# One level of a blocked triangular inverse moved from TensorE to VectorE in a gated delta-rule kernel

## The chip, the cores and the metric

The kernel runs on one core of a Trainium2 chip. The metric is the device time of one execution in microseconds (us). All of the model is one launch; intermediate results that change their partition layout go through scratch tensors in DRAM.

## The reference, cut to what matters

The program is a chain of six residual blocks over 1024 tokens of width 256: a feed-forward block, windowed attention, two more feed-forward blocks, the gated delta-rule attention ("L1 attention") and a last feed-forward block. The change lies in the delta-rule attention, whose core is a scan over tokens, in 16 heads of 128 by 128 state:

```
q = l2norm(silu(conv(x @ Wq))) * DK**-0.5      # k likewise, v without the norm
g = exp(-softplus(x @ Wfa @ Wfb + dt_bias) * exp(A_log))
beta = sigmoid(x @ Wb)
def step(S, (qt, kt, vt, gt, bt)):
    S = S * gt[..., None]
    pred = einsum('bhk,bhkv->bhv', kt, S)
    delta = (vt - pred) * bt[..., None]
    S = S + kt[..., None] * delta[:, :, None, :]
    return S, einsum('bhk,bhkv->bhv', qt, S)
```

The kernel doesn't scan token by token. It takes chunks of 128 tokens. Inside a chunk the deltas solve a lower triangular system: with M the strictly lower matrix of decayed products of keys with keys, and the betas on the diagonal, delta = Z (v - k S), where Z is the inverse of the unit triangular matrix, scaled. Most of the kernel's second half is the making of M and of Z for each chunk and head.

## The kernel before

**Pairs.** The 16 heads are taken in 4 groups of 4 heads (`HG`), the 8 chunks in 4 pairs. That makes 16 pairs; a pair is one group of heads over 256 tokens, so it holds 2 chunks times 4 heads = 8 triangular matrices of 128 by 128.

**Stages of a pair,** each a Python generator whose `yield`s cut it into steps:

- `prepare`: convolutions of k and q (matmul L641, ScalarE L653, VectorE L655), their norms, the gates, and the products `kq` (L741, L742). It writes the betas over the norms, `cf`, to DRAM as `cfd` (L687), in elements of 4 bytes.
- `triangle`: M by levels n = 1, 2, 4, ... 64. A level makes the blocks of n rows below the diagonal blocks of n columns (matmul L791, L803), masks them into tiles (L854, L856, L857, or ScalarE copies), and moves the decay one level on (VectorE L813, GpSimd L819). Levels 1 to 8 go into the tile `ml`, level 16 into `mt16`, level 32 into `mt32`, level 64 into `mt64`. In the step of level 32, `ml` is written to DRAM as `dm` (L843, four transfers).
- `solve`: the 64 diagonal blocks of 16 by 16 (8 matrices times 8 blocks) are fetched from `dm` with one block per partition, `xb` (L888, eight transfers of 8 partitions), scaled to `nb` (L899), and inverted by substitution on VectorE (L906 to L934). `zb` and its transpose `ztb` are written into two DRAM tensors `z` and `zt` (L949, sixteen transfers), which are read back with rows on partitions (L951, L954, six transfers).
- `invert`: levels 16 and 32 on TensorE with the same code: `pmz` = M^T z (L968), negated by ScalarE to `mz` (L976), two products `dz` (L983, L991), copied into `z` and `zt` (VectorE L1008, L1010 at level 16; ScalarE L1014, L1016 at level 32). Then level 64 (L1020, L1024, L1028, L1031).
- `values` and `gates`: v and the output gate.
- `advance` and `emit`: the state's recurrence over the two chunks of the pair (L1046 to L1078), the norm, and the output projection into `x` (L1085 to L1104). `advance` needs the pair's finished `zt` at `pw` (L1052).

**The order of the work.** The loop over i works on four pairs at once: `prepare` on pair i+2, `triangle` on pair i+1, `solve`, `invert`, `values`, `gates` on pair i, `advance` and `emit` on pair i-1. `weave` merges their steps: a lane (begin, end, n, steps) spreads n steps evenly between two fractions of the iteration. That merged order is what the program states; the framework then plans the engines' queues against a simulated timeline with priorities from that order, so an engine may take a later step early when the plan finds it idle. What it plans is fixed: on the chip each engine works through its queue in order. All DMAs are issued by one queue, SP's (SyncE).

**Buffers that matter.** The DRAM tensors `z` and `zt` and the tile `ml` exist twice, by parity of the pair (`turns`). Outside the blocks that are written they stay zero from the start. The pool `blk` (`diag`, `xb`, `nb`, `zb`, `ztb`) has one buffer each.

Of the kernel before, what the change touches and what calls it, by code (L numbers as in the profile page):

```python
# [10 lines left out]
F32 = mybir.dt.float32  # L11
# [497 lines left out]
def delta_rule(tc, a, x, xnT, pp, bc, kon, ones, kdw, first):  # L509
# [33 lines left out]
    with ExitStack() as ctx:  # L543
# [57 lines left out]
        for i in range(2):  # L601
            turn = {}
            for nm in ("ml", "mt16", "mt32"):
                turn[nm] = cst.tile([P, 2, HG, 64], F32, name=f"{nm}_{i}")
                nc.gpsimd.memset(turn[nm], 0.0)
            for nm in ("z", "zt"):
                turn[nm] = dram.tile([2, HG, P, P], F32, name=f"{nm}_{i}", bufs=1)
                for c in range(2):
                    for r in range(2):
                        nc.sync.dma_start(  # L610
                            out=turn[nm][c].rearrange("h r s -> r h s")[:, :, 64 * r : 64 * r + 64],
                            in_=turn["mt16"][:, c],
                        )
# [159 lines left out]
        def triangle(us):  # L773
# [11 lines left out]
            for i, n in enumerate(LEVELS):  # L785
# [43 lines left out]
                if n == 32:  # L829
# [8 lines left out]
                    for c, u in enumerate(us):  # L838

                        dm = u["dm"] = dram.tile([HG, P + 1, 64], F32, name="dm", bufs=4)  # L840
                        for half in (lo, hi):
                            r0 = half.start + half.start // 64
                            nc.sync.dma_start(  # L843
                                out=dm[:, r0 : r0 + 64, :].rearrange("h r s -> r h s"), in_=turn["ml"][half, c]
# [8 lines left out]
                if n < BLK:  # L853
                    nc.vector.copy_predicated(dst(flat(turn["ml"])), pred4, run4(pm[:, 0]))  # L854
                else:
                    nc.vector.tensor_mul(dst(flat(turn["mt16"])), run4(pm[:, 0]), run4(all_heads(mask)))  # L856
# [15 lines left out]
        def blocks(ap):  # L872
# [3 lines left out]
                tensor=ap.tensor, offset=ap.offset, ap=[[BLK * (pitch + 1), P // BLK], [pitch, BLK], [1, BLK]]  # L876
            )

        def solve(us, vb):
# [5 lines left out]
            for c, u in enumerate(us):  # L885
                for h in range(HG):
                    q0 = 32 * c + 8 * h
                    nc.sync.dma_start(  # L888
                        out=xb[q0 : q0 + 8].rearrange("b (i j) -> b i j", j=BLK),
                        in_=blocks(u["dm"][h]),  # L890
                    )
# [49 lines left out]
            )  # L941
            z = us[0]["z2"] = lev.tile([P, 2, HG, 64], F32, name="z", bufs=1)
            zt = us[0]["zt2"] = lev.tile([P, 2, HG, P], F32, name="zt", bufs=2)
            for c, u in enumerate(us):
                for got, to in ((zb, "z"), (ztb, "zt")):
                    full = u["p"]["turn"][to][c]
                    for h in range(HG):
                        q0 = 32 * c + 8 * h
# [312 lines left out]
```

## Time and profile before

| | |
|---|---|
| time, median of 3 runs | 1785.18 us (1783.14 to 1787.38) |
| the profiled execution | 1795.66 us, its span 1793.8 us |
| TensorE busy | 1532.6 us (85%), in 13152 matmul records (an f32 matmul leaves two) |
| VectorE busy | 1186.9 us (66%) |
| ScalarE busy | 831.3 us (46%) |
| GpSimd busy | 526.4 us (29%) |
| mean granted TensorE clock | 0.897 |
| DMA | 54.94 MB in 150348 packets, 116784 of them under 512 B |

In the page and in the answers below, PE is TensorE's matmul, PEld its weight load, DVE VectorE, ACT ScalarE, POOL GpSimd, SP SyncE. A group's row has the line, engine, operation, names (out<-in), shapes and count, then busy us and mean ns of one, then the engine's idle time just before it with what ended most of it. A row of waits has who waited for what, then us in total, how many times, and the longest. A row of the timeline has start, duration, engine, line, operation, names, shapes, count, and in brackets the idle time before it with its releaser. A row of windows has the stretch, its length, busy time of each engine with its number of instructions, granted clock (PEclk), DMA share and GB/s. The delta-rule attention runs from about 585 us to 1732 us of the span; the pairs follow each other there from about 664 us.

### The profile page before, as it was taken

What the parts mean: (1) busy time and instruction counts of PE and PEld (TensorE: products, weight loads), DVE (VectorE), ACT (ScalarE), POOL (GpSimd) and SP (SyncE); (2) the same over time, 40 slices, a digit from 0 to 9 for tenths busy, and PEclk for the clock granted to TensorE, in tenths of its full rate; (3) what the DMA queues carried; (4) which work ended last, traced back from release to release, by engine and by line L of the source; (5) the groups of instructions that cost most, each with busy time, mean ns of one, the idle gap of its engine ahead of it and who ended that gap; (6) DMA issues with size and microseconds to landing.
All of it is one profiled execution on the core that took longest, in us unless ns stands there. A gap on an engine that the chain in (4) does not pass through costs nothing.

```text
span 1793.8 us, 33380 instructions
## 1 busy us (share of the span) xinstructions
PE 1532.6 (85%) x13152; PEld 1107.1 (62%) x13152; DVE 1186.9 (66%) x2569; ACT 831.3 (46%) x1981; POOL 526.4 (29%) x470
## 2 busy tenths in 40 slices
PE   7886868777999766789989889898999898998879
PEld 3434445545555555667767677677778776776745
DVE  3999977584232357667678678876768877877221
ACT  2117273746122344536645645654665564563320
POOL 0022223231001034335434434433434442543100
PEclk9997989889999766789889989989889988989989
DMA  7020000002002001021111121102120120111100
GB/s 241 32 54 26 3 19 1 1 1 66 0 0 47 1 7 23 10 52 28 24 15 43 21 56 22 30 12 44 38 50 15 22 47 9 40 24 23 56 0 24
DMA packets 150348, 54.94 MB, mean 31 GB/s; under 512 B 116784, under 2 KB 142704, under 8 KB 149936
## 3 DMA queue, kind: packets, MB, share of 16 engines
q1 hardware_dynamic: 150192, 52.81, 12.8%
q8 instruction: 104, 1.70, 0.4%
q14 instruction: 52, 0.43, 0.1%
HBM read 39.11 MB, written 11.70 MB: 28 GB/s over the span
## 4 chain that ended last, share of the span: by engine, by line
PE 41%; DVE 26%; ACT 11%; DMA 9%; issue 6%; POOL 4%; SPq 3%; another core or an unknown queue 1%; DVEq 0%; POOLq 0%; ACTq 0%
PE ps L641 5%; DMA dm<-ml 4%; PE po L160 4%; PE pg L135 3%; PE pu L135 3%; DVE kq L813 3%; ACT e L319 3%; PE pm L791 2%; PE pr L253 2%; DVE k L655 2%; PE pg L700 2%; PE px L1101 2%; DVE other L195 2%; PE po L365 2%; DVE other L208 2%
## 5 line engine op out<-in xcount | busy, mean ns | idle before, releaser
L819 POOL TENSOR_TENSOR k<-k,d 128x512 f32<-128x512 f32 x96 | 149.7, 1559 | 312.2 <-PE pm L791 190.6
L791 PE MATMUL pm<-kq,k 128*64 128x64 f32 x3072 | 133.5, 235 | 29.9 <-POOL kq L742 11.5
L791 PEld LDWEIGHTS pm<-kq,k 128*64 128x64 f32 x3072 | 113.3, 146 | 62.0 <-issue 40.0
L813 DVE TENSOR_TENSOR kq<-kq,d 128x1024 f32<-128x1024 f32 x96 | 130.8, 1363 | 17.8 <-PE pm L791 6.7
L319 ACT ACTIVATE e<-ps,nm 128x128 f32<-128x128 f32 x256 | 91.5, 397 | 63.6 <-DVE nm L314 62.3
L655 DVE SCALAR_TENSOR_TENSOR k<-ps,pp,k 128x256 f32<-128x256 f32 x192 | 84.7, 473 | 27.0 <-ACT k L653 25.5
L655 DVE SCALAR_TENSOR_TENSOR q<-ps,pp,q 128x256 f32<-128x256 f32 x192 | 86.2, 478 | 22.7 <-ACT q L653 20.0
L655 DVE SCALAR_TENSOR_TENSOR v<-ps,pp,v 128x256 f32<-128x256 f32 x192 | 87.5, 474 | 19.8 <-ACT v L653 18.5
L253 PE MATMUL pr<-xnT,wq 128*128 128x512 f32 x128 | 64.7, 641 | 22.1 <-DVE nm L314 10.6
L641 PE MATMUL ps<-xnT,wv 128*128 128x259 f32 x256 | 79.5, 439 | 2.7 <-DVE v L655 1.5
L983 PE MATMUL dz<-mz,zt 64*64 64x32 f32 x768 | 74.9, 230 | 8.0 <-ACT mz L976 8.0
L991 PE MATMUL dz<-zt,mz 64*64 64x32 f32 x1024 | 81.4, 234 | 0.0
L641 PE MATMUL ps<-xnT,wq 128*128 128x259 f32 x256 | 78.6, 442 | 0.4 <-DVE ss L681 0.2
L365 PE MATMUL po<-wo,oT 128*128 128x256 f32 x256 | 64.1, 394 | 13.7 <-ACT oT L362 12.4
L991 PEld LDWEIGHTS dz<-zt,mz 64*64 64x64 f32 x1024 | 67.3, 147 | 12.4 <-issue 10.6
L1101 PE MATMUL px<-wdo,oT 128*128 128x256 f32 x256 | 70.4, 421 | 5.1 <-ACT oT L1097 5.1
L641 PE MATMUL ps<-xnT,wk 128*128 128x259 f32 x256 | 71.8, 418 | 1.0 <-ACT k L653 0.5
L742 POOL TENSOR_TENSOR kq<-q,ge 128x1024 f32<-128x1024 f32 x16 | 51.3, 3209 | 70.3 <-PE pso L1073 40.0
L653 ACT ACTIVATE q<-ps,pp 128x256 f32<-128x256 f32 x64 | 30.4, 474 | 89.1 <-PE ps L641 86.5
L968 PE MATMUL pmz<-z,mt 64*64 64x64 f32 x1024 | 56.1, 233 | 18.0 <-DMA z<-z 13.7
L968 PEld LDWEIGHTS pmz<-z,mt 64*64 64x64 f32 x1024 | 42.9, 140 | 44.4 <-issue 17.8
L708 ACT ACTIVATE gy<-pg,pp 128x256 f32<-128x256 f32 x64 | 29.4, 474 | 85.4 <-PE pg L700 67.5
(215 smaller groups left out, 3953.5 us busy)
## 6 DMA issues: line engine op xcount, KB each, us to landing
zt<-zt SPq DMA_DIRECT2D x32, 256.0 KB
dm<-ml SPq DMA_DIRECT2D x64, 64.0 KB
z<-z SPq DMA_DIRECT2D x64, 64.0 KB
wq<-in_aWq SPq DMA_DIRECT2D x1, 2048.0 KB
wo<-in_aWo SPq DMA_DIRECT2D x1, 2048.0 KB
wk<-in_dWk SPq DMA_DIRECT2D x4, 512.0 KB
wq<-in_dWq SPq DMA_DIRECT2D x4, 512.0 KB
wv<-in_dWv SPq DMA_DIRECT2D x4, 512.0 KB
```

What stands on the lines that cost most here:

```text
L135: nc.tensor.matmul(ps[:n], lhsT=w[:, c, cs], rhs=xnT[:, c, cols], start=(c == 0), stop=(c == KC - 1))
L253: nc.tensor.matmul(pr, lhsT=w[:, c, hcol : hcol + HD], rhs=xnT[:, c, PAD + hf * 512 : PAD + (hf + 1) * 512], start=(c == 0), stop=(c == KC ...
L319: nc.scalar.activation(e[:, s, j, :], ps[:, s, j, :], AF.Exp, bias=nm[:, 4 * s + j : 4 * s + j + 1], scale=SUB**-0.5, accum_out=z[:, s, j ...
L365: nc.tensor.matmul(po, lhsT=oT[:, h, :], rhs=wpool["wo"][:, g * HG + h, :], start=(h == 0), stop=(h == HG - 1),)
L641: nc.tensor.matmul(ps[:, 0 : 2 * P + 3], lhsT=w[nm][:, c, h * HD : (h + 1) * HD], rhs=xnT[:, c, PAD + t0 - 3 : PAD + t0 + 2 * P], start=(c ...
L655: nc.vector.scalar_tensor_tensor(yh, xi, pp[:, col : col + 1], yh, ALU.mult, ALU.add)
L791: nc.tensor.matmul(pm[half, :, c * HG + h, :].rearrange("p b (s l) -> p b s l", l=n), lhsT=k[:, c, h, half], rhs=rights(kq[:, :, c, h, half]),
L813: nc.vector.tensor_mul(kqr, kqr, dl.unsqueeze(1).unsqueeze(3).to_broadcast([P, 2, 2 * HG * runs, n]),)
L819: nc.gpsimd.tensor_mul(kl, kl, dr.unsqueeze(2).to_broadcast([P, 2 * HG * runs, n]))
L968: nc.tensor.matmul(pmz[half, c, h], lhsT=p["turn"][f"mt{n}"][half, c, h], rhs=z[half, c, h], start=True, stop=True,)
L991: nc.tensor.matmul(runs(dz[half, 1, c, h]), lhsT=mz[half, c, h], rhs=right(zt[half, c, h, half], n), start=True, stop=True,)
L1101: nc.tensor.matmul(px, lhsT=oT[:, h, :], rhs=u["w"]["o"][:, h, :], start=(h == 0), stop=(h == HG - 1))
```

## The change

Level 16 of the inverse leaves TensorE. Each of the 64 pairs of neighbouring 16 by 16 blocks becomes 32 joins (8 matrices times 4), and VectorE makes them right behind the substitution, on 128 partitions: 32 joins times 4 quarters of the columns. For a join with diagonal inverses z1, z2 and the block m of M between them, the new block is -z2 m z1.

- `mt16` is gone; level 16 of M is masked into `ml` with a copy like levels 1 to 8, so that it reaches DRAM in `dm`, which now comes behind level 16.
- `dm` is one tensor for both chunks, with a pitch that lets one access pattern step through all blocks: `xb` is one transfer instead of eight. Four more transfers fetch the blocks m, once for each quarter, into `mb` (rows of 16 floats, 64 B).
- At the end of `solve`, z1 (a quarter of the columns of `ztb`) and z2 are copied from SBUF to SBUF onto the 128 partitions (eight transfers), and `zb` and `ztb` are written to DRAM in one transfer each.
- A new stage `join` has two products and two reductions on VectorE over 1024 elements each, two small ScalarE operations for the sign, and eight transfers that write the new blocks into `zt` (rows of 64 B) and `z` (rows of 4 floats, 16 B). The six transfers that read `z` and `zt` back follow it.
- `invert` keeps level 32 (in its own short code) and level 64: 5 steps instead of 8.
- The lanes get other places.

```diff
@@ delta_rule @@
-            for nm in ("ml", "mt16", "mt32"):
+            for nm in ("ml", "mt32"):
...
-                turn[nm] = dram.tile([2, HG, P, P], F32, name=f"{nm}_{i}", bufs=1)
+                turn[nm] = dram.tile([2 * HG, P + 1, P], F32, name=f"{nm}_{i}", bufs=1)
...
@@ triangle @@
-                        dm = u["dm"] = dram.tile([HG, P + 1, 64], F32, name="dm", bufs=4)
+                    dm = us[0]["dm"] = dram.tile([2 * HG, P + 2, 64], F32, name="dm", bufs=2)
...
-                if n < BLK:
-                    nc.vector.copy_predicated(dst(flat(turn["ml"])), pred4, run4(pm[:, 0]))
-                else:
-                    nc.vector.tensor_mul(dst(flat(turn["mt16"])), run4(pm[:, 0]), run4(all_heads(mask)))
+                nc.vector.copy_predicated(dst(flat(turn["ml"])), pred4, run4(pm[:, 0]))
@@ solve @@
-            for c, u in enumerate(us):
-                for h in range(HG):
-                    q0 = 32 * c + 8 * h
-                    nc.sync.dma_start(
-                        out=xb[q0 : q0 + 8].rearrange("b (i j) -> b i j", j=BLK),
-                        in_=blocks(u["dm"][h]),
-                    )
+            dm = us[0]["dm"]
+            nc.sync.dma_start(
+                out=xb.rearrange("b (i j) -> b i j", j=BLK),
+                in_=blocks(dm, (BLK, BLK, 64), (1, 0, BLK), (0, 1, BLK)),
+            )
+            mb = blk.tile([P, BLK, BLK], F32, name="mb")
+            for j in range(4):
+                nc.sync.dma_start(
+                    out=mb[32 * j : 32 * j + 32],
+                    in_=blocks(dm, (32, 32, 32), (1, 0, BLK), (0, 1, BLK), col=BLK),
+                )
...
+            for j in range(4):
+                at = slice(32 * j, 32 * j + 32)
+                nc.sync.dma_start(out=z1[at], in_=ztb[0:64:2, 4 * j : 4 * j + 4, :])
+                nc.sync.dma_start(out=z2[at], in_=zb[1:64:2])
+            rows = ((BLK, BLK, 64), (1, 0, BLK), (0, 1, BLK))
+            for got, to in ((zb, "z"), (ztb, "zt")):
+                nc.sync.dma_start(out=blocks(us[0]["p"]["turn"][to], *rows), in_=got)
+            us[0]["blocks"] = mb, z1, z2
+            yield
@@ join, new @@
+            nc.vector.tensor_mul(
+                four,
+                mb.rearrange("p r s -> p s r").unsqueeze(1).to_broadcast([P, 4, BLK, BLK]),
+                z1.unsqueeze(2).to_broadcast([P, 4, BLK, BLK]),
+            )
+            yield
+            nc.vector.tensor_reduce(mz1, four, AX.X, ALU.add)
+            yield
+            nc.vector.tensor_mul(
+                four,
+                z2.unsqueeze(1).to_broadcast([P, 4, BLK, BLK]),
+                mz1.unsqueeze(2).to_broadcast([P, 4, BLK, BLK]),
+            )
+            yield
+            nc.vector.tensor_reduce(add, four, AX.X, ALU.add)
+            nc.scalar.mul(z21, add.rearrange("p j i -> p i j"), -1.0)
+            nc.scalar.mul(zt21, add, -1.0)
+            yield
+            for j in range(4):
+                at = slice(32 * j, 32 * j + 32)
+                nc.sync.dma_start(
+                    out=blocks(turn["zt"], (32, 32, 32), (1, 0, 4), (0, 1, BLK), row=4 * j, col=BLK), in_=zt21[at]
+                )
+                nc.sync.dma_start(
+                    out=blocks(turn["z"], (32, 32, 32), (1, 0, BLK), (0, 1, 4), row=BLK, col=4 * j), in_=z21[at]
+                )
...
@@ the loop over pairs @@
-                lanes.append((0.5, 0.8, 12, chain(advance(past[0]), emit(past[0]), advance(past[1]), emit(past[1]))))
+                lanes.append((0.0, 0.35, 12, chain(advance(past[0]), emit(past[0]), advance(past[1]), emit(past[1]))))
...
-                lanes.append((0.1, 0.2, 14, solve(now, vbs[i % 2])))
-                lanes.append((0.3, 0.95, 8, invert(now)))
-                lanes.append((0.55, 0.7, 7, values(now)))
+                lanes.append((0.15, 0.2, 14, solve(now, vbs[i % 2])))
+                lanes.append((0.2, 0.35, 5, join(now)))
+                lanes.append((0.5, 0.9, 5, invert(now)))
+                lanes.append((0.05, 0.45, 7, values(now)))
...
-                lanes.append((0.2, 0.85, 9, triangle(mid)))
+                lanes.append((0.15, 0.75, 9, triangle(mid)))
...
-                lanes.append((0.0, 0.3, 21, prepare(ahead)))
+                lanes.append((0.0, 1.0, 21, prepare(ahead)))
```

## The prediction

> **What bounds the kernel now.** I read the page's busy row and chain first, then the windows of the delta-rule stretch, the waits of its engines, SP's and VectorE's timelines around the longest wait, the groups that the change removes or resembles, and the end of the stretch.
>
> ```profile
> PE 1532.6 (85%) x13152; PEld 1107.1 (62%) x13152; DVE 1186.9 (66%) x2569; ACT 831.3 (46%) x1981; POOL 526.4 (29%) x470
> PE 41%; DVE 26%; ACT 11%; DMA 9%; issue 6%; POOL 4%; SPq 3%; another core or an unknown queue 1%; DVEq 0%; POOLq 0%; ACTq 0%
> ```
> ```profile
> 664.00:1624.00 960.00, 858.25 (x10024) 690.53 (x10026) 716.14 (x1404) 528.96 (x911) 395.16 (x341) 0.89 0.16 29
> 1252.00:1258.00 6.00, 3.33 (x26) 2.50 (x26) 0.00 (x0) 2.62 (x8) 0.00 (x0) 0.61 0.09 10
> 1258.00:1264.00 6.00, 4.21 (x30) 2.68 (x32) 5.22 (x16) 1.52 (x3) 3.64 (x3) 0.50 0.00 0
> ```
> ```profile
> DVE nb L899 <- DMA xb<-dm: 84.7, 15, 10.5
> PE pmz L968 <- DMA z<-z: 9.7, 7, 3.8
> ```
> ```profile
> 1241.36 2.11 SPq L843 DMA_DIRECT2D dm<-ml  x2
> 1243.57 0.56 SPq L687 DMA_DIRECT2D cfd<-cf  x1
> 1244.18 1.28 SPq L843 DMA_DIRECT2D dm<-ml  x2
> 1245.56 11.42 SPq L888 DMA_DIRECT2D xb<-dm  x8
> 1258.58 0.42 DVE L899 SCALAR_TENSOR_TENSOR nb<-xb,diag 64x256 f32<-64x256 f32 x1 [10.49 <-DMA xb<-dm]
> ```
>
> The 960 us from 664 to 1624 hold 15 pairs; the transfers `dm` of successive pairs are issued 63.9 us apart (727.95 to 1622.31 over 14). Per pair TensorE is busy 57.2 us (858.25/15), VectorE 47.7, and VectorE stands still another 5.6 (84.7/15) for `xb`. TensorE leads, VectorE with its DMA wait (53.4) is close behind, and the chain goes through both. The waits are uneven: in four pairs (about 919, 986, 1244, 1499 us) `cfd` is issued between the halves of `dm` and the wait is about 10 us, as shown; the other eleven average 4. The stop costs twice: VectorE does nothing from 1252 to 1258, and TensorE's granted clock is 0.61, then 0.50.
>
> **What leaves TensorE.** Per pair level 16 has 16 products `pmz` and 32 products `dz`, in records 32 and 64.
>
> ```profile
> 1164.31 0.68 PE L968 MATMUL pmz<-z,mt 64*64 64x64 f32 x16
> 1164.92 1.15 PE L791 MATMUL pm<-kq,k 128*64 128x64 f32 x32
> 1166.00 0.30 PE L983 MATMUL dz<-mz,zt 64*64 64x32 f32 x4
> ```
>
> Two prices. The groups' busy time: half of L968's 56.1 us, two thirds of L983's 74.9, half of L991's 81.4, together 119 us or 7.4 us a pair. From start to start: 16 `pmz` in 0.61 us, so 1.2 us for 32; the 64 `dz`, four every 0.115 us from 1166.00 on, 1.9 us; together 3.1 us at full clock, 3.5 at the stage's 0.89. The Trainium skill ("Trainium Kernel Development and Optimization", Performance Expectations) says that a matmul's busy time is a poor measure because matmuls are pipelined. I follow it: 3.4 us a pair, not 7.4. TensorE falls to 53.8 us. Over 16 pairs that is 54 us, and 119 by the other reading. ScalarE loses one `mz` (0.6 us) and gains two small operations, which I put at 0.3 each from its 128x256 rows at 0.47: nothing.
>
> **What VectorE gets.**
>
> ```profile
> L741 DVE TENSOR_TENSOR kq<-k,ge 128x1024 f32<-128x1024 f32 x16 | 21.5, 1344 | 15.5 <-PE pso L1073 15.4 <-ACT ge L722 0.2
> L920 DVE TENSOR_TENSOR tmp<-nb,vb 64x512 f32<-64x512 f32 x16 | 18.4, 1148 | 0.4
> L313 DVE TENSOR_REDUCE nm<-ps 128x8 f32<-128x1024 f32 x32 | 38.5, 1210 | 0.4 <-PE ps L302 0.3
> L1010 DVE COPY_PREDICATED zt<-kon,dz 64x256 f32<-64x256 int32 x32 | 13.7, 427 | 0.2
> L1008 DVE COPY_PREDICATED z<-kon,dz 128x256 f32<-128x256 int32 x16 | 7.0, 436 | 4.8 <-remote 2.8 <-PE dz L991 1.9
> ```
>
> The product with `z2` is L741's shape: 1.35 us. The product with `mb` reads one operand in strides of 16 floats. Below it lies L741, above it twice L920 (both operands strided), 2.3; I take 1.6. A reduction of 1024 is L313's 1.21, or twice L926's 0.67; I take 1.25, twice. Sum 5.45 us (4.9 to 6.5). Gone are L1008 (0.44), two L1010 (0.85) and L856 (0.41); the masked copy of level 16 adds 0.57 (L854). Net 4.3 us a pair (3.8 to 5.4): VectorE goes to 52.0.
>
> **Transfers and waits.** SP issues 36 transfers a pair before (`cfd` 1, `dm` 4, `diag` 1, `xb` 8, writes 16, reads 6), and 35 after (1, 4, 1, 1, `mb` 4, z1 and z2 8, writes 2 and 8, reads 6): issue time doesn't change.
>
> `xb` is one issue of about 0.4 us instead of eight of 0.32. That can take up to 2.2 us off the wait, less where the first four went out before `dm` had landed; a single transfer of all 1024 runs could land later, so from -2.2 to +1. Behind `nb` stands all of VectorE's queue, and behind that TensorE (`pm`, `pq`). `dm` now follows level 16's mask, some 3.5 us later (in one pair the mask of level 8 starts at 1119.63, of level 16 at 1123.15). That delays `solve`, not VectorE, if the queue has other work there.
>
> The new wait is z1's. From the last substitution: `ztb` on GpSimd 1.2 us (L939), seven issues of 0.34, then about 1.9 for the last to land (a `z<-zb` issue ended at 1648.02 and landed by 1650.01): 5.5 us. Bounds are 0, if the queue holds 5.5 us of other lanes' work, and 5.5. The nearest row is the wait for `xb`, also one fetch straight in front of its reader, at 3 to 4 us in calm pairs; with `zb` and one neighbour's operation in between I take 2.5. Queued behind it are the triangle's `kq` and the convolutions, on which TensorE and ScalarE wait.
>
> The writes behind `join` are 8 issues and a landing, 4.6 us by the same row, covered by the gap between `join`'s end at 0.35 of the iteration and `invert`'s start at 0.5, some 9.6 us. If the plan closes that gap, TensorE waits at `pmz` as before (L968).
>
> **The order.** `cfd` (step 15 of 21) moves from 0.21 of the iteration to 0.69, `dm` (step 6 of 9) from 0.60 to 0.52: in the stated order `cfd` now comes behind `dm`. That speaks for calm waits at `xb`; I take 3.0 us a pair for 5.6. `prepare` moves to low priority; its convolutions feed everything two pairs later, so nothing waits at once. `values` and `triangle` move earlier and cost nothing unless VectorE, which carries them, is full: then their work shows whole. At the end of the stretch the earlier `advance` counts:
>
> ```profile
> 1684.33 0.58 ACT L1031 COPY zt<-dz 64x512 f32<-64x512 f32 x1 [0.48 <-PE dz L1028]
> 1697.09 1.05 PE L1046 MATMUL psr<-s,kq 128*128 128x128 f32 x8
> 1698.92 1.16 PE L1052 MATMUL pw<-r,zt 128*128 128x128 f32 x8 [0.78 <-DVE r L1048]
> ```
>
> The last pair's `zt` is finished at 1684.9, but its `pw` starts at 1698.9, behind the pair before it. With that pair half an iteration earlier up to 14 us go; I take 8, as its work must fit elsewhere.
>
> **The sum.** VectorE: 52.0 + 3.0 + 2.5 = 57.5 us a pair, now above TensorE's 53.8. Before, the leading engine (57.2) was 6.7 us under the period. VectorE's other waits (on ScalarE and TensorE, 10.6 us a pair) should shrink as those engines get ahead of it; I leave 5. Period 62.5, 1.4 less: 22 us over 16 pairs, and 8 at the end: 30 us. The profiled execution took 1795.7 us, 10.5 above the median of the runs: 1765.7 there, 1755 as a median. This case I give 0.41, with its own range 1735 to 1775.
>
> **The rivals.**
>
> *The join stops VectorE (0.27, slower).* z1's 5.5 us lie bare in every pair, `xb` keeps 4: 52.0 + 5.5 + 4 + 5 = 66.5 us, 2.6 more than now; 42 us less 8: 1819. For it: `nb` shows that the plan puts a reader close behind its fetch. Against it: `ztb` and `zb` are ready early, and many lanes have VectorE work. It decides once the two waits pass 6.9 us a pair (63.9 - 52.0 - 5).
>
> *The 16-byte runs hold the queue (0.11, slower).* `join` writes 2048 runs of 16 B a pair. By `cfd` (1024 runs of 4 B), which kept the half of `dm` behind it out for 10.7 us instead of 3.3 in a calm pair, they cost 15 us, 5 beyond the gap, for which TensorE waits at level 32: 80 - 30 = 50 us slower, 1835. The skill ("DMA: Bandwidth & Descriptors", Specifications) speaks against this change too: under 512 B an engine reads, modifies and writes. But the 64 B runs into the same tensors, which that rule would damn as well, land 1.9 us after issue; I take that row for the sum, as these runs too lie in different rows.
>
> *TensorE stays the bound and the collisions end (0.15, faster).* 53.8 + 6.7 = 60.5: 54 us, the whole 14 at the end, and about 20 from the clock, which falls to half for 12 us after each of four stops (6 us each): 88 us, 1697. Against it: VectorE's load.
>
> *The change doesn't show (0.07).* The planner packs the old gaps again, and what TensorE saves returns as waits on VectorE: 1785.
>
> **How the numbers follow.** A measurement of this kernel tells some 0.2% (3.6 us) from nothing. Main case and third rival give faster: 0.55. The last gives 0.07 within, the first two 0.38 slower. The range 1700 to 1825 reaches over the main case and the first rival to the edges of the others.
>
> **What would show it.** Right: matmul records fall by 1536; VectorE's busy time rises by 60 to 85 us; the wait `nb <- xb` falls to 40 to 55 us in all; a wait of the join's first product on z1 of about 40; less than 14 us between the last `zt` and its `pw`; a period of 62 to 63. Wrong: VectorE's waits for DMA together over 110 us (first rival), a wait of level 32's `pmz` for z over 60 us (second), or a granted clock in the stretch above 0.93 with TensorE's share unchanged (third).

## The result, and the profile after

The changed kernel takes 1797.14 us (median of 6 runs, 1793.21 to 1803.5) against 1784.44 us for the kernel before on the same chip (6 runs, 1780.55 to 1787.38): ratio 1.007, 95% interval 1.0049 to 1.0091. It is slower by 0.7%, where the forecast was 1.7% faster. The profiled executions happen to lie together (1793.21 us after, 3.9 below its median; 1795.66 before, 11 above the median of these runs), so the difference is looked for in the stretch that was changed, not in the spans.

The page's busy row and its chain, after:

```profile
PE 1447.1 (81%) x11616; PEld 1052.2 (59%) x11616; DVE 1250.0 (70%) x2585; ACT 821.8 (46%) x1997; POOL 533.1 (30%) x468
PE 44%; DVE 29%; ACT 9%; issue 7%; DMA 5%; SPq 3%; POOL 3%; DVEq 0%; ACTq 0%; POOLq 0%
```

TensorE lost 1536 records and 85 us of busy time; VectorE gained 63 us. On the chain of work that ended last, DMA fell from 9 to 5%, and VectorE rose from 26 to 29%. The window of the 15 pairs (busy of PE, PEld, DVE, ACT, POOL, then granted clock, DMA share, GB/s):

```profile
664.00:1624.00 960.00, 779.28 (x8493) 638.89 (x8491) 774.24 (x1417) 520.90 (x927) 405.18 (x342) 0.87 0.20 35
```

The issues of `dm` in successive pairs now lie 65.2 us apart (724.85 to 1637.7 over 14), against 63.9 before. The same window, read as 65.2 us a pair: VectorE is busy 52.6 (774.24/960 x 65.2), TensorE 52.9, so the two are level. What they wait for there (total us, times, longest; VectorE's answers first, then TensorE's):

```profile
DVE gy L723 <- ACT ge L721: 38.0, 13, 4.2
DVE nb L910 <- DMA xb<-dm: 24.0, 13, 2.8
...
DVE four L971 <- DMA z<-ztb: 3.7, 2, 3.1
...
PE pm L794 <- DVE kq L744: 47.6, 12, 7.9
PE pm L794 <- POOL kq L745: 21.4, 2, 11.4
PE pm L794 <- DVE kq L816: 20.7, 11, 3.9
...
PE pmz L1020 <- DMA z<-z: 14.6, 6, 9.3
```

The wait for `xb` fell from 84.7 to 24.0 us, and the new wait for z1 is only 3.7: the transfers do what was hoped. New is TensorE's wait for `kq` L744, 47.6 us, a row that the kernel before does not have. TensorE stands still 12.3 us a pair (180.72/960 x 65.2), before 6.8. The groups, by shape (count, then busy us, mean ns, idle before):

```profile
L971 DVE TENSOR_TENSOR four<-mb,z 128x1024 f32<-128x1024 f32 x15 | 29.7, 1982 | 3.7 <-DMA z<-ztb 3.7
L744 DVE TENSOR_TENSOR kq<-k,ge 128x1024 f32<-128x1024 f32 x15 | 31.9, 2129 | 0.1
L980 DVE TENSOR_TENSOR four<-z,mz 128x1024 f32<-128x1024 f32 x15 | 23.2, 1545 | 0.0
L978 DVE TENSOR_REDUCE mz<-four 128x64 f32<-128x1024 f32 x15 | 18.1, 1207 | 0.0
L987 DVE TENSOR_REDUCE add<-four 128x64 f32<-128x1024 f32 x15 | 18.0, 1198 | 0.0
```

The join takes 5.93 us a pair (the 64 diagonal blocks of a pair make 32 pairs of neighbours, one join each). And `kq`, 1.34 us before, now takes 2.13 in a queue whose order has changed; the last section says what it waits for inside that time. VectorE's timeline in one pair shows the place (start, duration, and in brackets the idle time before it), and after it TensorE's in the same stretch:

```profile
1076.48 0.53 DVE L948 TENSOR_TENSOR zb<-vb,diag 64x256 f32<-64x256 f32 x1
1078.04 0.69 DVE L739 TENSOR_TENSOR qk<-pq,kon 128x512 f32<-128x512 f32 x1 [1.03 <-PE pq L735]
1082.51 1.22 DVE L723 SCALAR_TENSOR_TENSOR gy<-gy,ge 128x1024 f32<-128x1024 f32 x1 [3.78 <-ACT ge L721]
1083.65 2.04 DVE L658 SCALAR_TENSOR_TENSOR k<-ps,pp,k 128x256 f32<-128x256 f32 x5
1085.62 1.92 DVE L971 TENSOR_TENSOR four<-mb,z 128x1024 f32<-128x1024 f32 x1
...
1088.44 2.35 DVE L744 TENSOR_TENSOR kq<-k,ge 128x1024 f32<-128x1024 f32 x1
1090.71 0.47 DVE L658 SCALAR_TENSOR_TENSOR v<-ps,pp,v 128x256 f32<-128x256 f32 x1
1091.11 1.20 DVE L978 TENSOR_REDUCE mz<-four 128x64 f32<-128x1024 f32 x1
```
```profile
1088.58 1.14 PE L644 MATMUL ps<-xnT,wv 128*128 128x259 f32 x4 [1.03 <-DVE k L658]
1090.94 1.15 PE L794 MATMUL pm<-kq,k 128*64 128x64 f32 x32 [1.21 <-DVE kq L744]
1095.94 1.97 PE L794 MATMUL pm<-kq,k 128*64 128x64 f32 x32 [3.85 <-DVE kq L816]
1099.07 2.06 PE L644 MATMUL ps<-xnT,wk 128*128 128x259 f32 x4 [1.16 <-DVE v L658]
```

In this pair VectorE has holes until 1082.5, in which it waits for ScalarE's gates and TensorE's products. From then on it is solid to 1111, and the join stands in that solid part, among the operations that release TensorE's next product each time.

At the end of the stretch:

```profile
1694.33 0.58 ACT L1057 COPY zt<-dz 64x512 f32<-64x512 f32 x1 [1.23 <-PE dz L1054]
...
1694.97 1.16 PE L1078 MATMUL pw<-r,zt 128*128 128x128 f32 x8 [0.67 <-ACT zt L1057]
...
1724.77 5.42 PE L135 MATMUL pg<-xnT,w1g 128*128 128x512 f32 x12 [2.58 <-ACT sg L152]
```

The gap of 14 us between the last `zt` and its `pw` is gone. From the last `dm` to the last `px` it takes 93.7 us (1637.7 to 1731.40), before 104.7 (1622.31 to 1726.98). Another 6.8 us are saved behind that: from the last `px` to the end of the span it takes 60.0 us (to 1791.4), before 66.8 (to 1793.8). There the new plan has put more of the last feed-forward block's products (L135, shown) in front of the last `px`, into a wait of TensorE. So the end gives 17.8 us, and the last `dm` is 15.4 us later: in these two traces the pairs' loss and the end's gain nearly cancel.

### The profile page after: what moved, and what is told of

The parts are those of the page before. It is cut to its first block, busy times and chain, and to the rows that moved or that the text cites. A ratio compares the mean times of both kernels' runs of the same rounds, so it can differ in the third digit from the quotient of the medians.

```text
span 1791.4 us, 30359 instructions
## 1 busy us (share of the span) xinstructions
PE 1447.1 (81%) x11616; PEld 1052.2 (59%) x11616; DVE 1250.0 (70%) x2585; ACT 821.8 (46%) x1997; POOL 533.1 (30%) x468
## 4 chain that ended last, share of the span: by engine, by line
PE 44%; DVE 29%; ACT 9%; issue 7%; DMA 5%; SPq 3%; POOL 3%; DVEq 0%; ACTq 0%; POOLq 0%
PE ps L644 5%; PE pg L135 5%; PE po L160 4%; PE pu L135 4%; PE pm L794 3%; DVE kq L816 3%; PE px L1127 3%; ACT e L319 3%; DMA z<-z 2%; DVE k L658 2%; PE po L365 2%; PE pr L253 2%; PE pss L681 2%; DVE kq L744 2%; DVE four L971 1%
## 5 line engine op out<-in xcount | busy, mean ns | idle before, releaser
L794 PE MATMUL pm<-kq,k 128*64 128x64 f32 x3072 | 144.5, 252 | 113.2 <-DVE kq L744 47.6
L794 PEld LDWEIGHTS pm<-kq,k 128*64 128x64 f32 x3072 | 125.7, 162 | 152.7 <-issue 102.8
L822 POOL TENSOR_TENSOR k<-k,d 128x512 f32<-128x512 f32 x96 | 139.3, 1451 | 219.9 <-PE pm L794 149.9
L319 ACT ACTIVATE e<-ps,nm 128x128 f32<-128x128 f32 x256 | 91.3, 395 | 63.6 <-DVE nm L314 62.3
L644 PE MATMUL ps<-xnT,wk 128*128 128x259 f32 x256 | 84.2, 474 | 19.0 <-DVE k L658 12.4
L644 PEld LDWEIGHTS ps<-xnT,wk 128*128 128x128 f32 x256 | 55.3, 232 | 32.4 <-issue 8.2
L346 POOL TENSOR_TENSOR d<-d,dz 128x512 f32<-128x512 f32 x32 | 34.1, 1064 | 117.6 <-DVE dz L345 85.9
L644 PEld LDWEIGHTS ps<-xnT,wv 128*128 128x128 f32 x256 | 55.7, 235 | 20.5 <-issue 5.4
L1127 PEld LDWEIGHTS px<-wdo,oT 128*128 128x128 f32 x256 | 54.3, 221 | 21.8 <-ACT oT L1123 11.2
L365 PEld LDWEIGHTS po<-wo,oT 128*128 128x128 f32 x256 | 47.9, 194 | 29.7 <-ACT oT L362 17.9
L656 ACT ACTIVATE v<-ps,pp 128x256 f32<-128x256 f32 x64 | 29.9, 469 | 72.3 <-PE ps L644 72.1
```

What stands on the lines that cost most here:

```text
L319: nc.scalar.activation(e[:, s, j, :], ps[:, s, j, :], AF.Exp, bias=nm[:, 4 * s + j : 4 * s + j + 1], scale=SUB**-0.5, accum_out=z[:, s, j ...
L365: nc.tensor.matmul(po, lhsT=oT[:, h, :], rhs=wpool["wo"][:, g * HG + h, :], start=(h == 0), stop=(h == HG - 1),)
L644: nc.tensor.matmul(ps[:, 0 : 2 * P + 3], lhsT=w[nm][:, c, h * HD : (h + 1) * HD], rhs=xnT[:, c, PAD + t0 - 3 : PAD + t0 + 2 * P], start=(c ...
L656: nc.scalar.mul(yh, xi, pp[:, col : col + 1])
L794: nc.tensor.matmul(pm[half, :, c * HG + h, :].rearrange("p b (s l) -> p b s l", l=n), lhsT=k[:, c, h, half], rhs=rights(kq[:, :, c, h, half]),
L822: nc.gpsimd.tensor_mul(kl, kl, dr.unsqueeze(2).to_broadcast([P, 2 * HG * runs, n]))
```

## The experiments

Letters used in the expectations: A, the join's work on VectorE lies bare; B, the new order costs; C, TensorE's relief makes the gain; D, the join's latency costs. Ratios are to the kernel before on the same chip; VectorE's and TensorE's busy time are those of the whole profiled execution. An edit also makes the framework plan the queues anew, so two kernels differ in the order of their work too, unless it is said that they don't.

| run | what it is | us, median | ratio, 95% interval | VectorE | TensorE |
|---|---|---|---|---|---|
| change | | 1797.1 | 1.007 (1.0049 to 1.0091) | 1250.0 | 1447.1 |
| e1_old_order | change, lanes of before | 1947.0 | 1.0846 (1.0814 to 1.0878) | 1255.4 | 1523.9 |
| e2_before_new_order | before, lanes of the change | 1787.1 | 0.9969 (0.9948 to 0.999) | 1180.6 | 1500.1 |
| e3_no_join_math | change, no VectorE join | 1734.7 | 0.9675 (0.9631 to 0.9719) | 1160.3 | 1431.1 |
| e4_before_no16 | before, no level 16 | 1780.3 | 0.9936 (0.991 to 0.9961) | 1172.2 | 1466.6 |
| e5_level_back | change, level 16 on TensorE | 1797.5 | 1.0018 (0.9998 to 1.0038) | 1175.3 | 1540.4 |
| e6_second_on_gpsimd | one join product on GpSimd | 1834.7 | 1.0215 (1.0177 to 1.0253) | 1242.8 | 1448.6 |
| e7_values_late | values 0.5 to 0.9 | 1846.0 | 1.0244 (1.0195 to 1.0294) | 1250.9 | 1477.8 |
| e8_join_late | join 0.5 to 0.65 | 1814.7 | 1.0099 (1.0064 to 1.0134) | 1248.9 | 1466.8 |
| e9_join_unread | join made, not read | 1805.4 | 1.0071 (1.005 to 1.0092) | 1255.2 | 1455.6 |
| e10_no16_new_order | e4 in the new order | 1745.5 | 0.9752 (0.9704 to 0.9799) | 1162.6 | 1450.9 |
| e11_half_join | first half of the join | 1761.5 | 0.9818 (0.9788 to 0.9847) | 1210.5 | 1432.8 |
| e12_nudge | change, a lane by 0.01 | 1801.8 | 1.006 (1.004 to 1.008) | 1245.0 | 1445.9 |
| e13_more_on_scalar | change, 2.7 us to ScalarE | 1794.4 | 1.0089 (1.0057 to 1.0122) | 1213.9 | 1444.0 |
| e14_prepare_early | change, prepare 0 to 0.3 | 1868.5 | 1.0488 (1.0459 to 1.0518) | 1268.4 | 1495.0 |
| e15_past_late | change, advance 0.5 to 0.8 | 1821.2 | 1.0238 (1.0202 to 1.0274) | 1253.7 | 1478.0 |
| e16_before_more_on_scalar | e2, 2.7 us to ScalarE | 1738.6 | 0.9764 (0.9733 to 0.9795) | 1157.3 | 1484.7 |
| e17_join_behind_kq | change, join behind kq | 1845.8 | 1.0343 (1.0309 to 1.0377) | 1252.6 | 1488.1 |
| e18_behind_kq_and_scalar | e17 and e13 | 1813.0 | 1.0177 (1.0145 to 1.0208) | 1231.0 | 1455.9 |

### The order by itself

The lanes of the one kernel are given to the other, and nothing else is edited. Only `invert`, which has a level more in the kernel before, didn't get the very same place everywhere: in the new order it stands at 0.25 to 0.9 in e2 and e16, 0.3 to 0.9 in e5, and 0.5 to 0.9 in e10 and the change. In the changed kernel (the join from 0.2 to 0.3 there):

```
-  advance, emit (0.0, 0.35)   solve (0.15, 0.2)   join (0.2, 0.35)   invert (0.5, 0.9)
-  values (0.05, 0.45)         triangle (0.15, 0.75)                  prepare (0.0, 1.0)
+  advance, emit (0.5, 0.8)    solve (0.1, 0.2)    join (0.2, 0.3)    invert (0.3, 0.95)
+  values (0.55, 0.7)          triangle (0.2, 0.85)                   prepare (0.0, 0.3)
```

> The changed kernel with the lanes of the kernel before (join between 0.2 and 0.3, all else as before). Theory A (VectorE is full: the join's 5.9 us a pair and its clash with GpSimd are bare, wherever the steps stand): within 15 us of the changed kernel's 1797. Theory B (the new order is to blame: with prepare spread over the iteration, kq comes late and TensorE waits for it): 20 to 50 us less, 1745 to 1777, and the wait of pm on L744 falls under 15 us. Theory C (the chain of transfers around the join is to blame): no change either, but with larger waits for DMA.

> The kernel before with the lanes of the changed one (invert, which keeps level 16 and its 8 steps, from 0.25 to 0.9). A: within 10 us of 1784. B: 15 to 40 us slower, 1800 to 1824, with TensorE waiting for kq. C: within 10 us of 1784; cfd no longer between the halves of dm, so the wait of nb on xb falls from 85 us under 60 under each theory.

In the kernel before, the order is worth 0.3%; in the changed one, going back to the old one costs 7.8%. So B falls; for e1 no theory expected a loss of that kind. What the new order does with the waits is seen in the waits of VectorE of e2:

```profile
DVE gy L720 <- ACT ge L718: 56.3, 14, 9.6
DVE nb L899 <- DMA xb<-dm: 24.6, 8, 5.9
```

The wait for `xb` falls by 60 us (from 84.7), as far as in the changed kernel and without its coalesced transfers (the many small issues merged into few). But the wait of `gy` rises by 46 (from 10.4). Most of the removed wait came back at another place, and the median moved by 5 us.

### The join's operations

e3 leaves out the two products and two reductions on VectorE, e11 the second of each, and e9 makes all four and reads none of their results; z1, z2 or the first half's result go where the joined block went:

```
 e3:  -nc.vector.tensor_mul(four, mb, z1)  -tensor_reduce(mz1, four)
      -nc.vector.tensor_mul(four, z2, mz1) -tensor_reduce(add, four)
 e3, e9:  -nc.scalar.mul(z21, add, -1.0)   +nc.scalar.mul(z21, z2[:, :, 0:4], -1.0)
          -nc.scalar.mul(zt21, add, -1.0)  +nc.scalar.mul(zt21, z1, -1.0)
```

> The changed kernel without the join's four VectorE operations; its transfers, its two ScalarE operations and its steps stay, and what it writes is z1 and a part of z2 in place of the joined block. A: 60 to 95 us less than 1797 (5.9 us in each of 16 pairs), 1702 to 1737. B: 15 to 40 us less. C: less than 15 us.

> The changed kernel with all four join operations on VectorE, but their result unread: z1 and a part of z2 are written in place of the joined block, as in the kernel without join operations (1735). A (load: VectorE's 5.9 us a pair lie bare): as slow as the change, 1795 to 1815. D (latency: what waits behind the join's result is what costs): as fast as without the join, 1735 to 1750. Between the two: the share of each.

> The changed kernel with only the first product and the first reduction of the join (3.2 of its 5.9 us on VectorE); their result is written in place of the joined block. A (each microsecond of VectorE counts): 1735 plus 70 times 3.2 over 5.9, 1765 to 1782. If it is a matter of a threshold (VectorE has room for a part): under 1750, or, the other way, above 1790.

The windows of e3, e11, e9 and e2, in this order, columns as above:

```profile
664.00:1624.00 960.00, 811.52 (x8980) 667.48 (x8981) 722.99 (x1432) 542.87 (x975) 425.72 (x356) 0.90 0.22 39
```
```profile
664.00:1624.00 960.00, 789.48 (x8824) 650.90 (x8824) 766.37 (x1454) 536.39 (x960) 426.86 (x353) 0.91 0.21 38
```
```profile
664.00:1624.00 960.00, 776.12 (x8436) 634.63 (x8436) 770.71 (x1404) 514.38 (x921) 415.69 (x341) 0.87 0.20 35
```
```profile
664.00:1624.00 960.00, 848.07 (x10210) 698.74 (x10211) 724.88 (x1434) 533.59 (x935) 415.70 (x349) 0.91 0.16 30
```

Without the join TensorE does 8980 records in the window, with it 8436, read or not. The join costs 0.0395 of the time (1.007 - 0.9675), 70 us, 4.4 of its 5.93 us a pair. As the unread join costs the same, it is the load on VectorE and not the wait for its result: A holds, D falls. The first half costs 26 us and the second 45, for 50 and 40 us of VectorE (1210.5 - 1160.3, 1250.0 - 1210.5); on its own chip e11 was 1761.5, just under A's range.

Where the halves went is seen when a pair is split up: the period (from the issues of `dm`, as above), VectorE's busy time, its waits for DMA, and its other waits, which are the rest. The last three are the window's, scaled to the period:

| | period | busy | waits for DMA | other waits |
|---|---|---|---|---|
| before | 63.9 | 47.7 | 5.6 | 10.6 |
| e2, new order alone | 63.6 | 48.0 | 1.6 | 13.9 |
| e3, change without join | 61.0 | 45.9 | 1.2 | 13.9 |
| e11, first half | 62.9 | 50.2 | 2.1 | 10.6 |
| change | 65.2 | 52.6 | 2.0 | 10.6 |
| e9, all of it, unread | 66.4 | 53.3 | 2.4 | 10.7 |

The new order raises the other waits by 3.3 us, and the join's first half takes these 3.3 away again: that much of it is hidden. The second half takes nothing more away and lengthens the pair in full. (Each row is one execution; those of e2, e3 and e11 were 15, 8 and 6 us under their medians.)

How much a new plan alone can move was to be shown by a control:

> A control: the changed kernel with the substitution's place moved by a hundredth of a turn (0.16 to 0.21 for 0.15 to 0.2). Every edit makes the framework plan all queues anew; this shows how much a new plan alone moves the time. If the single differences between these kernels can be read as causes: within 5 us of the change, 1800 to 1812. If plans scatter: off by 10 to 30 us in either direction, and no difference of that size between two of the kernels means much.

1.006 against 1.007, but this says nothing about new plans: the nudge left the plan as it was. In the traces VectorE's 2585, ScalarE's 1997 and GpSimd's 468 instructions and SP's issues come in the same order as in the changed kernel, and TensorE's records too but for two places. It shows that a kernel repeats its time. The better control is e9: only 1584 of its 2585 VectorE instructions stand at the same place in the queue as in the change, and the time is the same. On the other side e7 and e17 below do the same VectorE work in other places and are 1.7 and 2.7% slower than the change. So the join's 4%, with e11 between and e9 as the repeat, is well supported; a single difference of 1 or 2% is not by itself a cause.

### TensorE's side

> The kernel before without level 16 of the inverse (no pmz, dz, mz and masked copies of that level; the mask of level 16 into mt16 stays), so what TensorE's relief is worth when nothing is put in its place. A: 30 to 60 us less than 1784 (TensorE 3.4 us, VectorE 1.3 us a pair, and the chain of invert shorter). B: the same. If it is under 15 us, TensorE was no bound at all, and the relief had nothing to give.

> The kernel before without level 16 of the inverse (its products, the results' copies; the masked product stays), in the new order, with the many small transfers of before. In the old order this was 1780, 12 us under before; without the join, with the new order and the coalesced transfers, 1735. If the order is what lets TensorE's relief show: 1735 to 1750. If the coalesced transfers are: 1770 to 1785.

> The changed kernel with level 16 back on TensorE as before (masked product, two rounds of products and the copies of its results), without the join and without the transfers that feed it and carry its result; the coalesced transfers (one read of the key blocks, one write for each of z and zt) and the new order stay. A (VectorE's join is what the change pays for; the transfers and the order are what it gains): the kernel without join operations took 1735, and level 16 on TensorE was worth 12 us when it was left out before, so 1745 to 1755, about 35 faster than before and 50 faster than the change. Rival C (the 1735 came from TensorE's relief, which only shows once the order is new): level 16 costs its full 54 us there, so 1780 to 1795, no gain over before.

```
 e4, e10:  -for n in (16, 32):                  +for n in (32,):
 e5:       +mt16 mask, +for n in (16, 32):      -mb, z1, z2, join, z21, zt21
```

Leaving level 16 out is worth 0.6% in the old order, 12 us where 30 to 60 were expected, and 2.2% in the new one (0.9969 - 0.9752), and 3.4% (1.0018 - 0.9675, e5 to e3) with the coalesced transfers. e10 says that the order is what lets the removal show, nearly down to e3's time. e5 is what its rival C expected (no gain over before), not A: putting level 16 back costs 61 us instead of the 12 that e4 gave, so the low time of e3 did not come from the transfers and the order alone. The steps from before to change can now be added up, in parts of the time before: order -0.0031 (e2); coalesced transfers +0.0049 (e5 less e2); level 16 off TensorE, with the join's transfers, -0.0343 (e3 less e5); the join on VectorE +0.0395. The sum is +0.007, as it must be, since each step starts where the last one ended; with the steps in another order the terms would differ (level 16 alone is 0.6, 2.2 or 3.4%). Two large terms cancel.

### Moving the join, or taking load off VectorE elsewhere

> The changed kernel with the join's second product (1.55 us a pair on VectorE) on GpSimd. A (each microsecond of VectorE's join lies bare): 16 x 1.55 = 25 us off, less what VectorE loses while GpSimd's product runs (its k and q product went from 1.35 to 2.13 us beside one): 1780 to 1795. Rival D (the join's latency is what counts, not VectorE's load: TensorE waits for the chain behind it): GpSimd's product is slower by some 2 to 4 us a pair, so 10 to 40 us slower than the change, 1815 to 1845.

> The changed kernel with the seven steps of the value convolution moved from 0.05 to 0.45 of a turn to 0.5 to 0.9, where VectorE had 25 us of a pair broken by waits for ScalarE's gates; nothing is added or left out. A1 (the join costs because it stands in the stretch where VectorE is full already and TensorE waits for it): moving other VectorE work out of that stretch gives back 1 to 3 us a pair, so 1755 to 1790. A2 (VectorE's volume counts, wherever it stands): within 10 us of the change, 1795 to 1815.

> The changed kernel with the join itself moved from 0.2 to 0.35 of a turn to 0.5 to 0.65, and the levels 32 and 64 behind it to 0.7 to 0.98. A1: the join is then off the full stretch, 1 to 4 us a pair given back, 1740 to 1790. A2: within 10 us of the change, 1795 to 1815. Rival D (latency): the products of level 32 wait for it at the end of the turn, 1815 to 1850.

```
 e6:  -nc.vector.tensor_mul(four, z2, mz1)     +nc.gpsimd.tensor_mul(four, z2, mz1)
 e7:  -values (0.05, 0.45)                     +values (0.5, 0.9)
 e8:  -join (0.2, 0.35), invert (0.5, 0.9)     +join (0.5, 0.65), invert (0.7, 0.98)
```

None brought the gain that A or A1 hoped for. e6 fell into its rival D's range, e8 to the upper edge of A2's, e7 outside all. The moved product in e6:

```profile
L980 POOL TENSOR_TENSOR four<-z,mz 128x1024 f32<-128x1024 f32 x14 | 39.9, 2849 | 22.5 <-DVE mz L978 22.5
```

GpSimd needs 2.85 us for what VectorE does in 1.55, and VectorE's busy time fell by 7 us in all instead of 25. So e6 took little load away and made the join later; it doesn't revive D, which e9 tests directly. e8 tests less than it was meant to: the plan's queue on VectorE has the join's first product in front of `kq` all the same, as its data are there early and the plan takes it when it finds VectorE idle. Within 5 us of the change it says nothing about the place. e7 is 31 us slower than the change (1.0244 - 1.007), so filling the apparent holes late in the turn did not help either.

> The changed kernel with other VectorE work taken off: the eight products of the transposed values with their norms and the sums of squares of the output, 1.37 and 1.35 us a pair on VectorE, are made by ScalarE (a scaled copy for each head; the square with its sum). A (VectorE's volume sets the time, whatever the operation): the join's runs gave 0.74 us of time for 1 us of VectorE, so 16 x 2.7 x 0.74 = 32 us off, 1765 to 1780, under both kernels. Rival (only the join's operations cost, or ScalarE's added 3 us a pair stand on the path): 1800 or more.

> The kernel before in the new order (1787) with the same 2.7 us a pair moved from VectorE to ScalarE. If TensorE leads there and VectorE has room: within 10 us, 1777 to 1797. If VectorE's volume counts there as much as after the change: 1750 to 1765.

```
-nc.vector.tensor_mul(u["vs"], ptv, over(u["kn"], P))
+for h in range(HG): nc.scalar.mul(u["vs"][:, h, :], ptv[:, h, :], u["kn"][:, h : h + 1])
-nc.scalar.square(sq, o); nc.vector.tensor_reduce(m, sq, AX.X, ALU.add)
+for h in range(HG): nc.scalar.activation(sq[:, h, :], o[:, h, :], AF.Square, accum_out=m[:, h : h + 1])
```

Both missed, in opposite directions: where the gain was expected there is none, and where it was in doubt it is larger than either theory had it. In the changed kernel it gives nothing (1.0089, interval over that of 1.007); in the kernel before with the new order it gives 2.05%, 37 us, and makes the best version of all that compute everything: 1738.6 us, ratio 0.9764. The page and the window of e16:

```profile
PE 1484.7 (86%) x13152; PEld 1085.8 (63%) x13152; DVE 1157.3 (67%) x2505; ACT 876.5 (51%) x2333; POOL 532.0 (31%) x470
```
```profile
664.00:1624.00 960.00, 861.18 (x10489) 711.26 (x10486) 720.55 (x1415) 596.99 (x1296) 417.48 (x355) 0.93 0.17 33
```

It bears on TensorE's side too. e16 moved some 43 us of VectorE's operations (16 x 2.7; the page's busy time falls by 23, as others got longer), left TensorE all its level 16, and gained 37 us. e10 took level 16 off TensorE and its masked copies, 21 us, off VectorE (busy 1180.6 to 1162.6), and gained 39. At e16's rate nearly half of what e10 gained can have been VectorE's part; no run separates the two. In a pair, e16's period is 2.4 us under e2's (61.2), with VectorE's busy time 2.1 less and its other waits nearly the same (13.6). In e13 the relief went into other waits:

```profile
DVE kq L817 <- PE pm L795: 39.1, 29, 3.8
DVE gy L723 <- ACT ge L721: 38.2, 13, 4.2
DVE nb L911 <- DMA xb<-dm: 35.1, 14, 4.7
...
PE pm L795 <- DVE kq L744: 43.4, 10, 6.9
```

TensorE's wait for `kq` L744 stays (43.4, in the change 47.6), and VectorE waits 23 us longer for `pm` and 11 longer for `xb`. A pair has 2.2 us less of VectorE's work (50.4) and 2.0 us more of its waits (11.8, and 2.8 for DMA).

### The place in VectorE's queue

That wait, which the change and e13 have (e9 a shorter one) and e2, e3, e5, e10 and e16 don't, made a last theory: the join's first product costs because it stands in front of `kq`. In e17 it uses the gate's buffer, and so comes behind `kq` in every pair:

```
-four = blk.tile([P, 4, BLK, BLK], F32, name="four")
+four = pre.tile([P, 4, BLK, BLK], F32, name="four", tag="tmp")
```

> The changed kernel with the join's products in the buffer that the gate's gy uses, nothing else: the join's first product then has to wait until the gate of the same turn is made, and the plan puts kq (L744), which the next triangle needs, in front of it on VectorE in every pair (before, behind it in nearly every pair). Moving the join's lane (the run with the join late) had not moved it in VectorE's queue at all. Theory Q (the join costs because it stands between the substitution and kq in VectorE's queue, so TensorE's next triangle starts later): TensorE's wait for kq L744, 47.6 us in 15 pairs, falls under 20, and the time falls by 20 to 45 us, ratio to before 0.980 to 0.996. Theory V (volume alone): the ratio stays at 1.00 to 1.01. Rival: the first square of the next pair's keys now waits for the join to give the buffer back, which delays the norms: over 1.01.

> The same, and the 2.7 us a pair of other VectorE work on ScalarE as in the run that gained nothing. Q: with kq in front of the join, VectorE's relief counts in the triangle's stretch as it did in the new order before the change (37 us): 15 to 35 us under the kernel without it, ratio 0.963 to 0.985. If the relief's failure had another cause (ScalarE's own load): within 5 us of the kernel without it.

Two groups and a wait of e17:

```profile
L971 DVE TENSOR_TENSOR four<-mb,z 128x1024 f32<-128x1024 f32 x14 | 50.2, 3587 | 0.0
L744 DVE TENSOR_TENSOR kq<-k,ge 128x1024 f32<-128x1024 f32 x14 | 17.2, 1225 | 5.5 <-ACT ge L725 5.4
...
PE ps L644 <- DVE k L658: 60.9, 21, 6.1
```

The profiled execution of e17 was its longest, 1867.9 us. The wait for `kq` is gone, as meant, and the time is 49 us longer than the change's (1.0343 - 1.007). TensorE now waits for the convolutions `k` behind the join (60.9 us, in the change 17.1), and the join's first product takes 3.59 us instead of 1.98 (3.43 in e18): 1.6 us a pair, 26 in all, because it now stands behind GpSimd's product (last section). e17 has yet another possible cost, the shared buffer, that it can't tell apart, so it is no clean test. e9 says more: there TensorE's wait for `kq` is 20.3 us, less than half of the change's, and the time is the same. So that place is not what the join costs. e18 gains 30 us on e17 by VectorE's relief that gained nothing in e13.

### Which lane of the old order hurts

> The changed kernel with one lane back in its old place: the 21 steps of prepare from 0.0 to 0.3 of a turn instead of 0.0 to 1.0. With all lanes in their old places it took 1947. If prepare's VectorE work is what collides with the substitution and the join: most of the 140 us, 1880 to 1950. If it is another lane: within 30 us of the change, 1790 to 1835.

> The changed kernel with another single lane back: advance and emit of the pair before from 0.5 to 0.8 instead of 0.0 to 0.35. If this lane makes the 140 us: 1880 to 1950; the recurrence then also waits at the end of the stretch, for which the old order paid up to 14 us: 1810 to 1830 if that is all.

`prepare` back at the front costs 4.2% over the change, `advance` back in the middle 1.7%; `values` late (e7, not quite its old place) 1.7%. Together 7.6%, close to the 7.8 of e1. So no single lane does it, and `prepare` has more than half. What `advance` costs lies at the end of the stretch: from the last `dm` to the end of the span e15 takes 178 us (1653.64 to 1831.6), the change 153.7. The change needs its new order: without it, it would have been 8.5% slower than before.

## Why the prediction was wrong, point by point

- *TensorE's relief, 3.4 us a pair.* As an amount of work it is about right: 52.9 us a pair (expected 53.8), 1536 records fewer. In the whole run TensorE's busy time fell by 85 us, between the two prices (54 and 119). That it would be felt is the doubtful part: 12 us in the old order, 39 to 61 in the new, and VectorE's masked copies have a share in that.
- *VectorE's load, 52.0 us a pair.* Right in the sum: 52.6, and +63 us in all (60 to 85 expected). The terms are less so: the join is 5.93 for 5.45 (the strided product 1.98 for 1.6, the second 1.55 for 1.35), and `kq`, which had no term, grew by 0.8.
- *The waits for transfers, 3.0 and 2.5.* Better than expected: 2.0 us a pair for both together (24.0 and 3.7, and 1.7 of `nb` for `mb`, by 65.2/960). The order is what shortens the wait for `xb` (e2). The rival of the 16-byte runs falls: TensorE waits 14.6 us for `z` in 15 pairs.
- *"VectorE's other waits (on ScalarE and TensorE, 10.6 us a pair) should shrink ...; I leave 5."* **This is the step that failed.** 65.2 - 52.6 - 2.0 = 10.6: from before to after they didn't shrink at all. This term alone is 5.6 us a pair too small; the transfers' waits were 3.5 too large and the load 0.6 too small, and 5.6 - 3.5 + 0.6 is the whole of the 2.7 us between 62.5 and 65.2. The prediction left out that a wait can move instead of ending: the new order took 4.0 us off the waits for DMA (5.6 to 1.6 in e2) and put 3.3 on the others (10.6 to 13.9). The join then did fill waits, as hoped, but only these 3.3, with its first half (e3, e11); the second half found none to fill (e11, the change, e9: 10.6 to 10.7). Why they stop at 10.6 in these kernels is not shown; e13 and most runs with other lanes have more.
- *The end, 8 us.* Too small: the gap between the last `zt` and its `pw` is gone, which with the rest up to `px` gives 11 us, and 6.8 more come behind it. The new order alone gives 8.4 of the 17.8 (e2: from the last `dm` at 1607.38 to the end of its span, 1770.5).
- *The sum.* The last `dm` comes 15.4 us later where some 20 us earlier were expected, and the end takes 17.8 us off where 8 stood. So the two traces differ by -2.4 us and the medians by +13: the execution traced before was 11 us above its median, the one after 3.9 below. That the time lies inside the range of 1700 to 1825 is no merit of the main case, as the range was drawn to reach over the first rival too. (The chances add up to 1.01; those for faster to 0.56.)
- *The rivals.* The right sign came from a mechanism that did not occur: z1 didn't stop VectorE (3.7 us). The third rival's clock did not come: it is 0.87 in the stretch, before 0.89. (Its half clock behind the four stops lasted some 6 to 17 us in the trace before, not 12 each.) Nearest was the case given 0.07, that what TensorE saves returns as waits: with level 16 left out and nothing put in its place (e4) the time fell by only 12 us. TensorE's busy time there is 53.0 us a pair, and its stops are 9.3 where they were 6.8.

What stays open: why 2.7 us a pair off VectorE is worth 37 us in the new order, nothing with the join, and 30 us with the join behind `kq`. The queues' order differs in each, and no run fixes it while the load alone changes. In e13, e16 and e18 ScalarE also takes over the reading of two results, so VectorE loses two of its waits with the work.

## What to carry to other kernels

Before moving work from the engine with the most busy time to the next one, take a little off each by itself: here 43 us of operations off VectorE, 66% busy, were worth about as much (37 us) as a whole level off TensorE, 85% busy, with 21 us of VectorE's copies (39 us). An engine's waits are room for new work only in part: of the join 3.3 us a pair went into waits, and the rest lengthened the pair. A forecast should say which wait will shrink and why, and otherwise let them stay. And test the order and the operation apart: the order alone made the kernel 0.3% faster, the change in the old order 8.5% slower, so neither half told what both would do.

## What the runs showed of the hardware

- In these traces a product of two tensors on VectorE that starts while a GpSimd operation runs nearly always ends a fixed time behind that operation, as if the two took turns. One pair of e17, VectorE's and GpSimd's rows, and GpSimd's product in the changed kernel's pair above:

```profile
1117.09 1.23 DVE L744 TENSOR_TENSOR kq<-k,ge 128x1024 f32<-128x1024 f32 x1 [0.25 <-ACT ge L725]
1118.23 3.95 DVE L971 TENSOR_TENSOR four<-mb,z 128x1024 f32<-128x1024 f32 x1
...
1117.13 3.38 POOL L745 TENSOR_TENSOR kq<-q,ge 128x1024 f32<-128x1024 f32 x1
```
```profile
1086.78 2.93 POOL L745 TENSOR_TENSOR kq<-q,ge 128x1024 f32<-128x1024 f32 x1 [10.04 <-ACT ge L725]
```

  In e17 `kq` starts 0.04 us ahead of GpSimd's product and takes 1.23. The join's first product starts in the middle of it and ends 1.66 us behind its end (1122.18 and 1120.51). In the changed kernel `kq` starts at 1088.44, inside GpSimd's product, and ends 1.08 us behind its end (1090.79 and 1089.71). It is so in nearly every pair: in the change 13 of the 16 `kq` start inside a GpSimd operation and each ends 1.08 us behind it, two that don't take 1.22 and 1.23, and one is an exception (1.22); in e17 14 of the 16 first products end 1.66 to 1.74 us behind, the other two take 1.87 and 1.88. The join's reductions, which read one tensor, take 1.18 to 1.22 us in the change wherever they start. So the strided first product costs 1.89 us alone (the mean of 14 in the change) and the second 1.23 (of 5); what is above that is time beside GpSimd. No run took GpSimd's operation away, so this rests on the timing alone.
- One issue that reads 1024 runs of 64 B (`xb`) and four that write 2048 runs of 16 B a pair cost no visible wait beyond those above; the coalescing itself brought no time (+0.0049, e5 less e2, in which `invert` starts a little later too).
- TensorE's busy time is not its amount of work: the same 11616 records took 1447.1 us in the change and 1523.9 in e1, where the granted clock of the stretch was 0.79 for 0.87.
